# Places and nodes of edges compared by TensorE and ScalarE: a graph layer's gather loop on one core

## The chip, the cores and the metric

The kernel runs on one core of a Trainium2 chip. Its time is the device time of one execution in microseconds (us), as the median of several; before the change it is 2077.98 us over 9 runs (2075.69 to 2081.77). Profiles come from one execution each, by the hardware profiler. In them PE is TensorE's matmuls, PEld its weight loads, DVE is VectorE, ACT ScalarE, POOL GpSimd and SP SyncE, which here only issues DMAs.

## The reference

There are N = 12500 nodes with D = 128 features and M = 200000 edges, sorted by their destination `dst`; each has a source `src` and a weight. The reference, cut to what matters:

```
h = relu(layernorm(x))
Qv, Ku = h @ W_Q.T, h @ W_K.T
score = einsum('md,md->m', Qv[dst], Ku[src]) / sqrt(D) * exp(-edge_weight)
# of each dst keep the 16 edges with the highest scores; softmax over them -> alpha
agg = segment_sum(alpha * (h[src] @ W_msg.T), dst)
out = x + relu(h @ W_self.T + agg)
```

## The kernel before

The edges are cut into G = 112 groups of GC = 14 chunks with P = 128 edges each. A group's edges end at some 112 nodes in a row, so all its work is on one window of 128 nodes. A group also reads the first chunk of the next one, since a node's edges can reach into it: NJ = 15 chunks.

**Preparation** (lines 240 to 397). `src`, `dst` and the edge weights are loaded as rows (`src_r`, `dst_r`, `ew_r`: 121 rows of CPR = 13 chunks) and turned by TensorE into columns (`to_columns`, L256), one column to a chunk: `idx_all` (the source of each edge), `dec_all` (exp of minus the weight), `pos_all` (an edge's place within its node, from a scan, L366) and `dlw` (its node counted from the window's start, less an offset of 8 per chunk). The rows of x come in six parts on SP's queue (L274), are normed (`row_stats`, `normed`, `finish`) and stored as the table `h_tab` (L327). GpSimd gathers the rows of the sources by indirect DMAs, one for each chunk of 128 edges (`gather`, L168 to 174): of the first RAW = 4 groups from x itself (they are normed on the chip later, L491 to 495), then from `h_tab`. A group's rows lie in a tile `hs`, of which there are 7. Groups 0 to 6 are all issued here, with `idx_all` as the index.

**The loop** (L684 to 752) runs `i` from -3 to 117 and in each iteration calls stages for different groups, from `i + 3` (loads) to `i - 5` (output). The order of the calls is the order of the instructions on each engine; nothing reorders them. The stages that matter here:

- `load_dst` (SP): 1920 destinations of the group as int32, broadcast to all 128 partitions (`dstb`, 960 KB, two buffers).
- `far_of` and `to_edges` (ScalarE): `far = (dst - node)^2` for 128 nodes by 1920 edges, then `to_e = relu(1 - far)`, a matrix of ones and zeros in bf16 that brings nodes' values to edges by matmul.
- `places` (VectorE, L530 to 536): two comparisons on 128 edges by 15 chunks by 40. `ow` is one where an edge's node in its chunk's window of 40 nodes is `w` (L533), `po` where its place is `k` (L535).
- `q_to_edges` (TensorE, 45 matmuls in four parts), then `scores` (VectorE, one fused product with the gathered row for each chunk, L556), `scores_in_slots` (`sl = po * s`, L564), `slots_by_node` (TensorE, 15 matmuls with `ow`, L571) and `best` (VectorE, the 16 highest of 40 places for each node, L582 to 597).
- `kept_to_edges`, `on_edges`, `weights` (`alz = ow * kept`, L636), `sums` (TensorE, L646, into the PSUM bank `a`), `sums_turned`, `products`, `output` (L666), `store`.
- `let_go` (L464 to 473): for two chunks at a time VectorE copies their indices to a small tile `ix` and GpSimd issues their gathers. `more(k)` (L695) spreads a group's seven calls over an iteration, from group 7 on. The seventh group after has the same `hs` buffer, so the calls come after `sums` of the group that had it.

The call of the two stages that the change moves most, in the loop:

```
at(i, q_to_edges, 1)
at(i + 1, far_of)
at(i - 1, slots_by_node)
at(i + 1, places)
...
at(i - 3, sums, 0)
at(i - 2, kept_to_edges)
```

Of the kernel before, what the change touches and what calls it, by code (L numbers as in the profile page):

```python
# [20 lines left out]
P = 128  # L21
# [55 lines left out]
def gnn_layer(  # L77
# [38 lines left out]
    CPR = 13  # L116
# [4 lines left out]
    assert RR <= P and RR - RF <= 1  # L121
# [22 lines left out]
    nvec = const.tile([P, 1], F32, name="nvec")  # L144
    a_qk = const.tile([P, P], F32, name="a_qk")
    wselfT = const.tile([P, P], F32, name="wselfT")
    wmsgT = const.tile([P, P], F32, name="wmsgT")

    idx_all = const.tile([P, CW], I32, name="idx_all")
    dec_all = const.tile([P, CW], F32, name="dec_all")  # L150
    pos_all = const.tile([P, CW], F32, name="pos_all")
    dlw = const.tile([P, G, NJ], F32, name="dlw")

    nb = const.tile([P, G], F32, name="nb")
# [13 lines left out]
    def gather(g, j0, j1, index, table=h_tab):  # L168
        if j0 == 0:
            T[g]["hs"] = rows_pool.tile([P, GC, D], F32, name="hs", bufs=7)  # L170
        for j in range(j0, j1):
            nc.gpsimd.indirect_dma_start(  # L172
                out=T[g]["hs"][:, j, :], out_offset=None, in_=table[0:N, :],
                in_offset=bass.IndirectOffsetOnAxis(ap=index(j), axis=0))
# [4 lines left out]
    def load_dst(g):  # L179
        n = chunks[g] * P  # L180
        lo = g * EG
        T[g]["dstb"] = dstb = rows_pool.tile([P, NJ * P], I32, name="dstb", bufs=2)
        hi = min(lo + n, M)
        if hi < lo + n:
            nc.vector.memset(dstb[:, hi - lo:n], 1 << 21)
        nc.sync.dma_start(dstb[:, 0:hi - lo], dst[lo:hi].partition_broadcast(P))
# [47 lines left out]
    with tc.tile_pool(name="edges", bufs=1) as ep, ExitStack() as stage:  # L234
        prep = stage.enter_context(tc.tile_pool(name="prep", bufs=1))
        RL = HALO + RW

        src_r = ep.tile([RR, RL], I32, name="src_r")
        h0 = src_r.bitcast(F32)
        h1 = alz[0][0:RR, 0:RL]  # L240
        dst_all = alz[1][:, 0:CW]
        assert max(RL, CW) <= NJ * (WW + STEP)
        dst_r = ep.tile([RR, HALO + RW], I32, name="dst_r")
# [5 lines left out]

        def load_rows(t, a):  # L250
            if RF:
                nc.scalar.dma_start(t[0:RF, 0:RW], a[0:RF * RW].rearrange("(p c) -> p c", c=RW))
            if REM:
                nc.scalar.dma_start(t[RF:RF + 1, 0:REM], a[RF * RW:M].rearrange("(p c) -> p c", p=1))

        def to_columns(rows, lo, put):  # L256

            for j0 in range(0, CPR, 4):
# [5 lines left out]
                put(lambda t: t[:, 0:RR * CPR].rearrange("e (p j) -> e j p", j=CPR)[:, j0:j1, :],  # L264
# [3 lines left out]
        nc.vector.memset(src_r, 0)  # L268
        load_rows(src_r, src)
        xs, t = [], 0  # L270
        for i, n in enumerate(sizes):
# [4 lines left out]
            t += n  # L276
        make_identity(nc, ident)
        nc.gpsimd.iota(dst_r, pattern=[[1, RL]], base=1 << 21, channel_multiplier=0)
        nc.gpsimd.memset(dst_r[0:1, 0:HALO], -1)
        nc.gpsimd.iota(slots, pattern=[[1, KM]], base=0, channel_multiplier=0,  # L280
# [3 lines left out]
        nc.vector.memset(ew_r, 0.0)  # L284
# [8 lines left out]
        nc.vector.memset(pos_all[:, RR * CPR:CW], 0.0)  # L293
        nc.vector.memset(dec_all[:, RR * CPR:CW], 0.0)
        nc.vector.memset(dst_all[:, RR * CPR:CW], float(1 << 21))
        for j in range(NJ):
            nc.vector.memset(w0[:, j:j + 1], float(lead(j)))
        for k in range(2):
            nc.vector.memset(sl1[k][:, :, KM:], 1.0)
# [5 lines left out]
        to_columns(src_f, 0, lambda at, p: nc.vector.tensor_copy(at(idx_all), p))  # L305
# [3 lines left out]
        def finish(i):  # L309
            t0, n, xg = xs[i]  # L310
            normed(xg, n, *stat[i])
            if i == 1:
                for t, w in zip(ws, (w_q, w_k, w_self, w_msg)):
                    nc.scalar.dma_start(t, w)
                nc.scalar.dma_start(b_i[:, 1:G],
                                    bass.AP(dst.tensor, dst.offset + EG - 1, [[EG, 1], [EG, G - 1]]))

                nc.scalar.dma_start(dst_r[0:1, HALO:], dst[0:RW].rearrange("(p c) -> p c", p=1))
                if RF > 1:
                    nc.scalar.dma_start(dst_r[1:RF, :], bass.AP(dst.tensor, dst.offset + RW - HALO,  # L320
                                                                [[RW, RF - 1], [1, RL]]))
                if REM:
                    nc.scalar.dma_start(dst_r[RF:RF + 1, 0:HALO + REM],
                                        dst[RF * RW - HALO:M].rearrange("(p c) -> p c", p=1))
                load_rows(ew_r, ew)
            for a, b in cuts:
                nc.sync.dma_start(by_part(h_tab)[a:b, t0:t0 + n, :], xg[a:b])  # L327
            if i == 1:
                load_dst(0)
# [6 lines left out]
        for g in range(RAW, min(7, G)):  # L336
            gather_at_once(g, h_tab)
# [18 lines left out]
        nc.vector.tensor_copy(row_i[:, 1, G - TAIL:G], row[:, 3, 0:TAIL])  # L356
        pb = bank("s", 1)
# [5 lines left out]
        nc.vector.tensor_copy(dst_f, dst_r)  # L363
        nc.vector.memset(h0[:, 0:1], 0.0)
        nc.vector.tensor_tensor(h0[:, 1:RL], dst_f[:, 1:RL], dst_f[:, 0:RL - 1], op=OP.is_equal)
        nc.vector.tensor_tensor_scan(h1, h0, h0, 0.0, op0=OP.mult, op1=OP.add)  # L366
        bb = rows_pool.tile([P, 2, G], F32, name="bb")
        nc.vector.tensor_copy(bb, pb[:, 0:2 * G].rearrange("p (a g) -> p a g", a=2))
        nc.vector.tensor_scalar(nb, bb[:, 0, :], nvec, -1.0, op0=OP.add, op1=OP.mult)
        to_columns(dst_f, HALO, lambda at, p: nc.scalar.copy(at(dst_all), p))  # L370
        to_columns(h1, HALO, lambda at, p: nc.scalar.copy(at(pos_all), p))
# [6 lines left out]
        for k in range(2):  # L378
            nc.vector.memset(alz[k], 0.0)
# [550 lines left out]
```

## Time and profile before

| what | value |
|---|---|
| median of 9 runs | 2077.98 us |
| the profiled execution: its own time | 2084.66 us |
| the profiled execution: span from first to last instruction | 2082.8 us |
| mean granted clock of TensorE | 0.797 |
| busy: TensorE, VectorE, ScalarE, GpSimd | 1305.4, 1499.1, 659.4, 1545.3 us |
| bytes moved by DMA | 253 MB, 107 MB of them the broadcast of `dst` |
| one iteration of the loop | about 18 us |

A line of the page's groups, or of the trace's answers by line, has the source line, the engine, the operation, output <- inputs with shapes and a count; after the first bar the busy time in us and the mean of one in ns; after the second the idle time of that engine just before these instructions, and what ended most of it (`issue` is time in which the engine waited for nothing that the profile shows). A line of the timeline has the start in us from the span's start, the duration, the engine and the operation; in brackets the idle time before it. A line of the waits has the waiting engine and tile, what it waited for, the total in us, how many times, and the longest. "Granted clock" is the share of TensorE's full clock that it was given.

### The profile page before, as it was taken

How to read it: one execution, taken by the hardware profiler on the slowest of the kernel's cores; microseconds unless marked ns; L12 is line 12 of the kernel's file. 1: busy time of each engine (PE TensorE's matmuls, PEld its weight loads, DVE VectorE, ACT ScalarE, POOL GpSimd, SP SyncE). 2: the span in 40 equal slices, each digit the busy share in tenths (PEclk: the TensorE clock that was granted, in tenths of full speed). 3: DMA queues.
4: the chain of work that ended last, by engine and by line, in shares of the span. 5: the costliest groups of instructions: out<-in, count | busy, mean ns of one | idle time of the engine just before them, and what ended most of it. 6: DMA issues, size and time to landing. Idle time of an engine off the chain costs nothing. (4 is left out here: it accounts for less than half of the span.)

```text
span 2082.8 us, 43581 instructions
## 1 busy us (share of the span) xinstructions
PE 1305.4 (63%) x14574; PEld 1205.1 (58%) x14575; DVE 1499.1 (72%) x7420; ACT 659.4 (32%) x1306; POOL 1545.3 (74%) x1578
## 2 busy tenths in 40 slices
PE   0267776666666666666666666666666666666664
PEld 0156776555556666555565566665565655566664
DVE  5688887777767777777777667777777777777764
ACT  4772333222223323232233223232222232233220
POOL 3777777777777777777777777777777777777772
PEclk9878888777777787787787777778778777777778
DMA  8743444333334444433433334434443333433420
GB/s 189 242 136 118 151 129 133 121 114 110 117 117 121 120 121 122 121 120 114 118 113 118 118 120 121 121 120 121 121 118 114 116 117 119 119 120 121 120 67 23
DMA packets 117572, 253.17 MB, mean 122 GB/s; under 512 B 32798, under 2 KB 76065, under 8 KB 116576
## 3 DMA queue, kind: packets, MB, share of 16 engines
q1 hardware_dynamic: 66104, 144.92, 20.1%
q0 software_dynamic: 50144, 102.74, 19.6%
q10 hardware_dynamic: 1094, 2.69, 0.6%
q8 instruction: 115, 1.88, 0.4%
q14 instruction: 115, 0.94, 0.1%
HBM read 236.40 MB, written 14.40 MB: 120 GB/s over the span
## 5 line engine op out<-in xcount | busy, mean ns | idle before, releaser
L172 POOL DMA_INDIRECT hs<-h_tab,ix x1465 | 1430.3, 976 | 446.8 <-issue 319.6
L556 DVE SCALAR_TENSOR_TENSOR prod<-hs,dec_all,q 128x128 f32<-128x128 f32 x1674 | 511.4, 344 | 257.9 <-DMA hs<-h_tab,ix 251.6
L546 PE MATMUL q<-q,to_e 128*128 128x128 bf16 x5022 | 463.8, 254 | 23.6 <-DVE prod L556 22.7
L654 PE MATMUL s<-ident,agn 128*128 128x128 f32 x112 | 48.4, 432 | 627.7 <-DVE kept L635 627.2
L546 PEld LDWEIGHTS <-to_e 128*128 128x128 bf16 x5022 | 410.4, 116 | 45.0 <-issue 28.9
L646 PE MATMUL a<-hs,alz 128*128 128x128 f32 x3348 | 423.4, 280 | 1.3 <-DVE alz L636 1.3
L646 PEld LDWEIGHTS a<-hs,alz 128*128 128x128 f32 x3348 | 401.5, 196 | 1.9 <-DVE alz L636 1.9
L654 PEld LDWEIGHTS s<-ident,agn 128*128 128x128 f32 x112 | 19.9, 178 | 643.9 <-issue 642.1
L571 PE MATMUL e<-ow,sl 128*41 128x40 f32 x3348 | 249.4, 264 | 2.0 <-DVE sl L564 2.0
L571 PEld LDWEIGHTS e<-ow,sl 128*41 128x41 f32 x3348 | 234.0, 183 | 16.8 <-DVE sl L564 2.1
L522 ACT ACTIVATE far<-dstb,nb 128x1920 bf16<-128x1920 int32 x112 | 212.9, 1901 | 0.0
L527 ACT ACTIVATE to_e<-far 128x1920 bf16<-128x1920 bf16 x112 | 201.2, 1797 | 0.0
L658 ACT COPY aggT<-s 128x128 f32<-128x128 f32 x112 | 29.8, 266 | 504.1 <-PE s L654 504.1
L585 DVE TENSOR_SCALAR ell<-slots,e 128x40 f32<-128x40 f32 x112 | 29.3, 261 | 201.6 <-PE e L571 195.2
L602 ACT ACTIVATE e<-v,km 128x16 f32<-128x16 f32 x112 | 34.5, 308 | 352.0 <-DVE km L594 352.0
L556 DVE DVE_READ_ACCUMULATOR prod<-hs,dec_all,q 128x1 f32 x1674 | 138.1, 82 | 0.2
L472 DVE COPY ix<-idx_all 128x2 int32<-128x2 int32 (+1 forms) x733 | 127.9, 174 | 12.8 <-DMA hs<-h_tab,ix 6.7
L631 ACT ACTIVATE up<-up 128x15 f32<-128x15 f32 x112 | 24.0, 215 | 297.3 <-DVE up L623 297.3
L651 ACT ACTIVATE agn<-a,rden 128x128 f32<-128x128 f32 x112 | 41.2, 368 | 208.0 <-PE a L646 208.0
L172 POOL DMA_INDIRECT hs<-in_x_dram,idx_all x56 | 63.2, 1129 | 43.9 <-DVE idx_all L305 20.9
L564 DVE TENSOR_TENSOR sl<-po,s 128x600 f32<-128x600 f32 x112 | 87.5, 781 | 3.9
L636 DVE TENSOR_TENSOR alz<-ow,kept 128x600 f32<-128x600 f32 x112 | 87.5, 781 | 3.8
(166 smaller groups left out, 1621.6 us busy)
## 6 DMA issues: line engine op xcount, KB each, us to landing
dstb<-in_dst_dram SPq DMA_DIRECT2D x111, 960.0 KB
hs<-h_tab,ix POOLq DMA_INDIRECT x1465
h_r<-h_tab SPq DMA_DIRECT2D x112, 64.0 KB
x_t<-in_x_dram SPq DMA_DIRECT2D x108, 64.0 KB
out_dram<-o SPq DMA_DIRECT2D x108, 64.0 KB
xg<-in_x_dram SPq DMA_DIRECT2D x2, 1400.0 KB
h_tab<-xg SPq DMA_DIRECT2D x2, 1400.0 KB
xg<-in_x_dram SPq DMA_DIRECT2D x1, 1120.0 KB
```

Source lines behind the costliest of these rows:

```text
L172: nc.gpsimd.indirect_dma_start(out=T[g]["hs"][:, j, :], out_offset=None, in_=table[0:N, :], in_offset=bass.IndirectOffsetOnAxis(ap=index(j ...
L472: nc.vector.tensor_copy(ix[:, j0:j1], idx_all[:, GC * g + j0:GC * g + j1])
L522: nc.scalar.activation(T[g]["far"][:, 0:n], T[g]["dstb"][:, 0:n], AF.Square, bias=nb[:, g:g + 1])
L527: nc.scalar.activation(T[g]["to_e"][:, 0:n], T[g]["far"][:, 0:n], AF.Relu, bias=1.0, scale=-1.0)
L546: nc.tensor.matmul(pq[:, (j - j0) * P:(j - j0 + 1) * P], lhsT=T[g]["to_e"][:, j * P:(j + 1) * P], rhs=upper(T[g]["q"][:, k, :]), start=(k ...
L556: nc.vector.scalar_tensor_tensor(prod, rows_of(g, j), dec_all[:, c:c + 1], T[g]["pq", b][:, (j % 4) * P:(j % 4 + 1) * P], op0=OP.mult, op1 ...
L564: nc.vector.tensor_tensor(sl1[g % 2][:, 0:n, 0:KM], T[g]["po"][:, 0:n, :], bc(T[g]["s"][:, 0:n], KM), op=OP.mult)
L571: nc.tensor.matmul(et[0:KM + 1, STEP * j:STEP * j + WN], lhsT=sl1[g % 2][:, j, :], rhs=T[g]["ow"][:, j, :], start=False, stop=(j == n - 1))
L636: nc.vector.tensor_tensor(alz[g % 2].rearrange("e (j w) -> e j w", w=WW + STEP)[:, 0:n, 0:WN], T[g]["ow"][:, 0:n, :], bc(kept[:, 0:n], WN) ...
L646: nc.tensor.matmul(T[g]["pa"][:, 0:P], lhsT=alz[g % 2][:, WW * j + PRE:WW * j + PRE + P], rhs=rows_of(g, j), start=(j == 0), stop=(j == n ...
L651: nc.scalar.activation(T[g]["agn"], T[g]["pa"][:, 0:P], AF.Copy, scale=T[g]["rden"])
L654: nc.tensor.transpose(so[:, 2 * P:3 * P], T[g]["agn"], ident)
```

## The change

- `src`, `dst` and the weights are now rows of CPR = 14 chunks, so that row `g` is group `g`: 112 rows. They are loaded on SP's queue in parts with a multiple of 16 rows and a rest (`sixteens`), `src` first, ahead of x; weights of the layer, `dst` and edge weights behind x. Before, they were on ScalarE's queue.
- `rel` holds each row's destinations relative to the last one of the row before, in bf16, on the chip. The broadcast `load_dst` is gone: `far_of` spreads row `g` to 128 partitions by a matmul with a column of the identity (four parts of up to 512 edges), and ScalarE squares it from PSUM.
- `places` no longer runs on VectorE. For each group one matmul turns 32 columns of `pd` (places and nodes of its 15 chunks), a copy by ScalarE takes them to `pdT`, three matmuls with a constant matrix `minus_at` give "own value less slot" for 2 x 15 x 40 slots, ScalarE squares each part (`away`) and at the end takes `relu(1 - square)` for all 1200 in one instruction. All these matmuls write the one bank `a`, which `sums` uses too.
- `slots_by_node` is cut in three, between the parts of `far_of`; `kept_to_edges` moves ahead of `sums`.
- There are 8 `hs` buffers and `let_go` is moved ahead by an iteration; groups 4 to 7 are let go in pieces too, group 4 within the preparation.

The core of the diff:

```diff
-    CPR = 13
+    CPR = GC
...
-    pos_all = const.tile([P, CW], F32, name="pos_all")
-    dlw = const.tile([P, G, NJ], F32, name="dlw")
...
+    pd = const.tile([P, G, 2, 16], BF16, name="pd")
+    dlw = pd[:, :, 1, 0:NJ]
+    minus_at = const.tile([32, 2, NJ, KM], BF16, name="minus_at")
...
-            T[g]["hs"] = rows_pool.tile([P, GC, D], F32, name="hs", bufs=7)
+            T[g]["hs"] = rows_pool.tile([P, GC, D], F32, name="hs", bufs=8)
...
-    def load_dst(g):
...
+        def sixteens(a, b):
+
+            m = b - (b - a) % 16
+            return [(p, q) for p, q in ((a, m), (m, b)) if p < q]
+
         def load_rows(t, a):
-            if RF:
-                nc.scalar.dma_start(t[0:RF, 0:RW], a[0:RF * RW].rearrange("(p c) -> p c", c=RW))
+            for p0, p1 in sixteens(0, RF):
+                nc.sync.dma_start(t[p0:p1, 0:RW], a[p0 * RW:p1 * RW].rearrange("(p c) -> p c", c=RW))
...
+        nc.gpsimd.memset(alz[1], 0.0)
...
-        nc.vector.memset(pos_all[:, RR * CPR:CW], 0.0)
+        nc.vector.memset(pd, 1.0)
...
+        for w in range(2):
+            nc.vector.tensor_scalar(kk[:, 0:1], nvec[0:32, :], -16.0 * w, None, op0=OP.add)
+            nc.vector.tensor_scalar(kk[:, 1:2], kk[:, 0:1], 15.0, None, op0=OP.is_equal)
+            nc.vector.tensor_scalar(eq, jj, kk[:, 0:1], None, op0=OP.is_equal)
+            nc.vector.scalar_tensor_tensor(minus_at[:, w, :, :], bm(slots[0:32, :], NJ), kk[:, 1:2], eq,
+                                           op0=OP.mult, op1=OP.subtract)
+        nc.vector.memset(alz[0], 0.0)
...
+        let_go(RAW, 1)
+        nc.vector.tensor_scalar(rel, dst_f[:, HALO:], dst_f[:, HALO - 1:HALO], 1.0, op0=OP.subtract, op1=OP.subtract)
+        let_go(RAW, 2)
...
-        byg = dst_all.rearrange("e (g j) -> e g j", j=GC)
-        nc.vector.tensor_sub(dlw[:, :, 0:GC], byg[:, 0:G, :], bc(bb[:, 0, :], GC))
-        nc.vector.tensor_sub(dlw[:, :, GC], byg[:, 1:G + 1, 0], bb[:, 0, :])
-        nc.vector.tensor_tensor(dlw, dlw, bm(w0, G), op=OP.subtract)
-        for k in range(2):
-            nc.vector.memset(alz[k], 0.0)
...
-        def far_of(g):
-            n = chunks[g] * P
-            T[g]["far"] = win.tile([P, NJ * P], BF16, name="far", bufs=1)
-            nc.scalar.activation(T[g]["far"][:, 0:n], T[g]["dstb"][:, 0:n], AF.Square, bias=nb[:, g:g + 1])
+        def far_of(g, b):
+            n0, n1 = 4 * P * b, min(4 * P * (b + 1), chunks[g] * P)
...
+            pr = bank("a", 1)
+            nc.tensor.matmul(pr[:, 0:n1 - n0], lhsT=upper(ident[0:RR, g:g + 1]).to_broadcast([RR, P]),
+                             rhs=rel[:, n0:n1], start=True, stop=True)
+            nc.scalar.activation(T[g]["far"][:, n0:n1], pr[:, 0:n1 - n0], AF.Square, bias=minus)
...
+        def edges_turned(g):
+            pr = bank("a", 1)
+            nc.tensor.matmul(pr[0:32, 0:P], lhsT=pd[:, g, :, :].rearrange("e w j -> e (w j)"), rhs=upper(ident),
+                             start=True, stop=True)
+            T[g]["pdT"] = win.tile([32, P], BF16, name="pdT")
+            nc.scalar.copy(T[g]["pdT"], pr[0:32, 0:P])
+
+        def away(g, b):
+            if b == 0:
+                T[g]["aw"] = win.tile([P, 2 * NJ * KM], BF16, name="aw")
+            n0, n1 = 400 * b, 400 * b + 400
+            pr = bank("a", 1)
+            nc.tensor.matmul(pr[:, 0:400], lhsT=T[g]["pdT"],
+                             rhs=minus_at.rearrange("k w j s -> k (w j s)")[:, n0:n1], start=True, stop=True)
+            nc.scalar.activation(T[g]["aw"][:, n0:n1], pr[:, 0:400], AF.Square)
+
         def places(g):
-            n = chunks[g]
-            T[g]["ow"] = win.tile([P, NJ, WN], F32, name="ow", bufs=5)
-            nc.vector.tensor_tensor(T[g]["ow"][:, 0:n, :], bm(slots, n), bc(dlw[:, g, 0:n], WN), op=OP.is_equal)
-            T[g]["po"] = win.tile([P, NJ, KM], F32, name="po", bufs=4)
-            nc.vector.tensor_tensor(T[g]["po"][:, 0:n, :], bm(slots, n),
-                                    bc(pos_all[:, GC * g:GC * g + n], KM), op=OP.is_equal)
+            T[g]["opo"] = win.tile([P, 2, NJ, KM], F32, name="opo", bufs=4)
+            nc.scalar.activation(T[g]["opo"].rearrange("e w j s -> e (w j s)"), T[g]["aw"], AF.Relu, bias=1.0,
+                                 scale=-1.0)
+            T[g]["po"], T[g]["ow"] = T[g]["opo"][:, 0], T[g]["opo"][:, 1]
...
-            if i + 2 > 0:
-                at(i + 2, load_dst)
...
-                g, k = (i + 3, k + 2) if k < 5 else (i + 4, k - 5)
-                if 7 <= g < G:
+                if i in (-1, 0, 1):
+                    g = i + 6
+                else:
+                    g, k = (i + 4, k + 2) if k < 5 else (i + 5, k - 5)
+                    if g < 8:
+                        return
+                if i >= -1 and g < G:
                     let_go(g, k)
 
             at(i, q_to_edges, 0)
+            at(i + 1, edges_turned)
             at(i - 5, output)
             at(i - 5, store)
             at(i - 3, weights)
             more(0)
             at(i - 4, sums_turned)
+            at(i + 1, far_of, 0)
             at(i - 4, sums_turned_out)
             at(i + 1, q_out)
             at(i, q_to_edges, 1)
-            at(i + 1, far_of)
-            at(i - 1, slots_by_node)
-            at(i + 1, places)
+            at(i + 1, far_of, 1)
+            at(i - 1, slots_by_node, 0)
+            at(i + 1, far_of, 2)
+            at(i - 1, slots_by_node, 1)
+            at(i + 1, far_of, 3)
+            at(i - 1, slots_by_node, 2)
+            at(i + 1, away, 0)
...
             at(i, q_to_edges, 2)
+            at(i + 1, away, 1)
             at(i + 2, h_turned)
+            at(i + 1, away, 2)
...
+            at(i - 2, kept_to_edges)
             at(i - 3, sums, 0)
-            at(i - 2, kept_to_edges)
...
             more(5)
+            at(i + 1, places)
```

## The prediction

> **What bounds the kernel now.** I read the page's busy line first, then the costliest groups, then GpSimd's instructions in order of time, and beside them VectorE's.
>
> ```profile
> PE 1305.4 (63%) x14574; PEld 1205.1 (58%) x14575; DVE 1499.1 (72%) x7420; ACT 659.4 (32%) x1306; POOL 1545.3 (74%) x1578
> ...
> L172 POOL DMA_INDIRECT hs<-h_tab,ix x1465 | 1430.3, 976 | 446.8 <-issue 319.6
> L556 DVE SCALAR_TENSOR_TENSOR prod<-hs,dec_all,q 128x128 f32<-128x128 f32 x1674 | 511.4, 344 | 257.9 <-DMA hs<-h_tab,ix 251.6
> ```
>
> No engine looks full. But the second row's idle time is 446.8/1465 = 0.305 us before every gather, and it is the same 0.30 to 0.31 us whatever the releaser: it belongs to the instruction. Busy plus idle is 1.281 us a gather, 1877 us for 1465 of them. The third row says that VectorE, when it waits, waits for gathered rows. So GpSimd's stream of 1563 gathers is the bound. It runs without a gap from 53 us to 2044.8 us.
>
> ```profile
> 1911.72 0.95 POOL L172 DMA_INDIRECT hs<-h_tab,ix  x1 [0.30 <-issue]
> ...
> 1912.92 0.78 DVE L533 TENSOR_TENSOR ow<-slots,dlw 128x600 f32<-128x600 f32 x1
> 1912.97 1.54 POOL L172 DMA_INDIRECT hs<-h_tab,ix  x1 [0.30 <-DVE alz L636]
> ...
> 1913.62 0.78 DVE L535 TENSOR_TENSOR po<-slots,pos_all 128x600 f32<-128x600 f32 x1
> ...
> 1914.82 0.95 POOL L172 DMA_INDIRECT hs<-h_tab,ix  x1 [0.30 <-issue]
> ...
> 1925.70 0.77 DVE L625 TENSOR_TENSOR mine<-x,po 128x600 f32<-128x600 f32 x1
> ...
> 1926.08 0.95 POOL L172 DMA_INDIRECT hs<-h_tab,ix  x1 [0.31 <-issue]
> ```
>
> An undisturbed gather takes 0.946 us, 1.2505 us from start to start. One in each iteration takes more. The one at 1912.97 began while VectorE ran L533 and then L535 without a break, and ended 0.11 us after L535. This holds over the whole trace: a gather that starts while a VectorE operation with two SBUF inputs runs ends at least 0.82 us after that operation; it loses the operation's remainder less 0.13 us. L625, as long but with one input in PSUM, delays nothing. I put every slow gather after 168 us to the operation that ended 0.82 us before its end: L533 and L535 together carry 37 us, all others 5. From the group row, all of it is 1430.3 - 1465 x 0.946 = 44 us.
>
> **The two ends.**
>
> ```profile
> 20.16 1.03 DVE L303 CAST src_r<-src_r 121x1664 f32<-121x1664 int32 x1 [14.30 <-DMA src_r<-in_src_dram]
> ...
> 24.24 1.12 POOL L172 DMA_INDIRECT hs<-in_x_dram,idx_all  x1 [20.94 <-DVE idx_all L305]
> ...
> 46.55 0.95 POOL L172 DMA_INDIRECT hs<-in_x_dram,idx_all  x1 [3.67 <-DMA hs<-in_x_dram,idx_all]
> ...
> 110.73 1.29 POOL L172 DMA_INDIRECT hs<-h_tab,idx_all  x1 [0.30 <-issue]
> ...
> 2043.86 0.95 POOL L172 DMA_INDIRECT hs<-h_tab,ix  x1 [0.30 <-DVE km L594]
> ```
>
> The first gather waits for the sources, which land at 20.16 us beside the x loads. The 57th, first of group 4, starts at 110.73, the last at 2043.86, and 38.9 us of drain follow. So the span is 110.7 + 1506 x 1.2505 (1883.3) + 49.9 of delays + 38.9 = 2082.8 us. The profiled execution took 2084.66, 1.9 us over its span and 0.3% over the median 2077.98.
>
> **The change, part by part.**
>
> *Sources first, by sixteens.* The first 0.8 MB of SP's queue is now src, ahead of x. At the 217 GB/s of the first 20 us that is 3.7 us of transfer[...]. VectorE was free at 5.9. It loses two clears (1.50 and 1.45) and gains the fill of pd (3584 elements at L268's 0.87 ns, 3.1), the constant matrix (per half two small operations of 0.15, a comparison of some 0.4, a fused one of 0.78: 3.0 in all), and one alz clear (2.06): free at 11.2. So the cast starts near 11.4, and with the old 4.1 us from cast to gather the first one starts near 15.5: 8.7 earlier. The next 56 took 86.5 us: 70.0 of cadence, 6.2 of waits for landings (42.9 to 53 us), 10.2 of delays by VectorE. The delays by L375 and L377 (2.4) go, the scan's and L380's stay. The waits for landings could vanish or double, as more gathers now run beside the x loads; I keep 6. Gather 57: 15.5 + 70 + 6 + 7.5 = 99, against 110.7.
>
> *SP's order.* The h_tab stores now queue behind weights, dst and ew. The x loads held SP until 35.6; 1.9 MB more at 0.2 MB a us makes 45, and 6.4 MB of stores at the 337 GB/s of 60 to 80 us take 19: h_tab is done near 70, and gather 57 doesn't want it before 99. Cost nothing; without these 29 us of cover, the difference one for one. Group 4's copies (21 more of 0.17 us) sit among VectorE's preparation, which ended at 90 and should end near 70.
>
> *Places.* L533 and L535 (1.56 us an iteration, 173 in all) leave VectorE. Of the busy time nothing is gained, VectorE waits for rows anyway; of the port, 37 us. Here the Trainium skill speaks against me. "SBUF — State Buffer", the section on the shared port pair, says that tensor_tensor was seen not to stall GpSimd's DMA, as descriptor generation needs the write interface (inferred there); and also that an operation with two SBUF inputs contends with a GpSimd instruction that reads SBUF. By the first the change gains 0 here, by the second 37. An indirect gather reads its indices from SBUF, and the two rows above fit the second: I take 37.
>
> *What remains.* L564 (sl) and L636 (alz), 0.78 each, and L516 (0.6 for two) still hold the port. They now miss the gather starts narrowly: sl ends at +0.04 us from a start, alz at -0.04, since both follow the landing of the iteration's last row. That order stays. From below: 0 if the phases hold. From above: at random phase a 0.78 us window costs 0.24 and L516 0.14, so 0.62 an iteration, 70 us. I take 0.1 an iteration over 100 iterations, nearer the trace, and 8 for the first ten, which took 11: 18 us.
>
> *far_of, away, edges_turned.* Eight matmuls and eight ScalarE reads through one PSUM bank, so each waits for the one before. ScalarE rows give 0.31 + 0.83 ns per element with a bias operand (L522, both sizes) and 0.20 + 0.83 without (L527): four reads of 512 at 0.74, three of 400 at 0.54, opo 1.2, one of 0.25, less 1.91 for the old far: +4 us, ScalarE from 5.4 to 9.4 us of an iteration. TensorE has this gap:
>
> ```profile
> PE s L654 <- DVE kept L635: 627.2, 110, 6.8
> ```
>
> 5.7 us an iteration in which it waits for VectorE's output. The new matmuls take some 2 us of it. What counts is the chain that begins there, after `output`: sums_turned and the first 512 columns to 0.9 us, ScalarE to 1.6 and with its two old copies to 2.1, three more rounds of about 1.0, slots_by_node finished between them: best can start at 5.0 to 5.5, where it started at 4.1. From there to the next output VectorE was busy for 10.7 (14.0 less 3.3 of waits for rows). The sum is 16.0, and on TensorE: away and its reads to 9.5, sums, the q products and the rest 6.7 more: 16.2. The gathers need 17.5. So it fits, with 1.3 to spare.
>
> Rule and row again: "TensorE: Matmul & The Clock Gate", the part on psum-queue depth-cycling, says that short stalls on a PSUM queue can make the clock oscillate between full and half. The row: granted clock 0.797, halves after the 5.7 us gap. With the gap filled I expect 0.9 or more and 16.2; by the rule at half clock, TensorE's 13 us of work at full would grow, and the chain with it to about 18.2.
>
> *dst no longer broadcast.* 107 MB in 111 loads leave SP's queue. No gather waits for a landing after 53 us, so 0; it could shift landings, thus phases (above).
>
> *Eight buffers, earlier release.* GpSimd's gaps are 0.30 throughout, so no buffer is waited for: 0. Group 8's first gather is due near 169; its copy comes late in iteration 3. The first iterations grow to some 21 us (ScalarE's 5.5 of raw_normed now delays away), which puts it near 153: 16 us of cover.
>
> **Sum.** 99 + 1883.3 + 18 + 38.9 = 2039.2 of span, 43.6 less than before's; on the median 2034. The drain has no places or far in it and stays.
>
> **Rivals.** (A) As summed: 2010 (no waits or delays) to 2050; 58%. (B) The phases shift and sl, alz or q_parts meet gather starts: up to 70 us in place of 18, 2050 to 2085, middle 2065; the bare 0.08 us of margin speaks for it, the fixed order against; 16%. (C) The places aren't the cause, something at the iteration's start is (SP issues there too): 45 us of delays remain, only the start is gained, 2060; L625's row and the exact ends speak against; 10%. (D) The one-bank chain outgrows 17.5 us: iteration 3 would start near 145, and 109 iterations plus 26 of drain give 2155 span at 18.2, about 2150. It loses from 17.6 on. For it: single buffer, eight hand-overs that no row of before shows. Against: the sum; 16%.
>
> Numbers: under 2010 I leave 3%, over 2090 13%; range 2010 to 2090. About 0.2% is what a measurement can tell from no change: faster 80% (A, C and most of B), same 5%, slower 15%.
>
> **What would show it.** Gathers of 1.5 us gone, the group mean near 953 ns (0.1 us an iteration); first gather near 15.5, the 57th near 99; TensorE's wait before sums_turned near 1 us, clock over 0.9; VectorE still waiting for rows. Wrong if gaps over 0.31 appear on GpSimd after 60 us (D, or a late copy), or if slow gathers stay, now ending after L564, L636 or L516 (B) or after none (C).

## The result, and the profile after

The changed kernel takes 2058.2 us (median of 10 runs, 2057.6 to 2061.5) beside 2077.0 us for the kernel before (31 runs, 2071.1 to 2081.8): ratio 0.9911, interval 0.9901 to 0.9921. It is faster by 18.8 us, where 43.6 were forecast. The profiled execution took 2056.25 us with a span of 2054.5. In fifteen of the eighteen runs below TensorE, VectorE and ScalarE paused again and again with nothing to wait for, and the kernel before took 2690 to 2716 us beside them: of those only durations of single instructions and the order within the drain are read; their times are given but nothing is concluded from them.

The page of the changed kernel, its busy line and the rows that answer to those of before:

```profile
PE 1642.6 (80%) x15474; PEld 1294.0 (63%) x15475; DVE 1329.0 (65%) x7222; ACT 1041.0 (51%) x2198; POOL 1511.6 (74%) x1580
...
L176 POOL DMA_INDIRECT hs<-h_tab,ix x1507 | 1443.2, 958 | 472.3 <-issue 296.6
L591 DVE SCALAR_TENSOR_TENSOR prod<-hs,dec_all,q 128x128 f32<-128x128 f32 x1674 | 497.6, 344 | 147.5 <-DMA hs<-h_tab,ix 126.8
...
L690 PE MATMUL s<-ident,agn 128*128 128x128 f32 x112 | 39.3, 351 | 134.1 <-DVE o L702 130.4
```

The mean of the gathers falls from 976 to 958 ns. Their delays are 1443.2 - 1507 x 0.946 = 17.6 us, where they were 44. VectorE still waits for rows, 126.8 us. TensorE's wait for VectorE just before sums_turned (L690, L654 before) falls from 627 to 130 us, 1.2 an iteration.

GpSimd's instructions in order of time, the five that carry the sum (start, duration, idle before):

```profile
15.76 1.12 POOL L176 DMA_INDIRECT hs<-in_x_dram,idx_all  x1 [9.58 <-DVE idx_all L338]
...
94.99 0.94 POOL L176 DMA_INDIRECT hs<-h_tab,ix  x1 [0.30 <-issue]
...
165.08 2.31 POOL L176 DMA_INDIRECT hs<-h_tab,ix  x1 [0.30 <-issue]
180.32 2.50 POOL L176 DMA_INDIRECT hs<-h_tab,ix  x1 [12.93 <-ACT up L667]
...
2009.28 0.94 POOL L176 DMA_INDIRECT hs<-h_tab,ix  x1 [0.30 <-DVE km L631]
```

The fourth line is new. GpSimd stands still for 12.93 us, and the gather after it waits 0.26 us longer than usual. The one at 180.32 is the first of group 8. Its index copies (L191) come at 178.36 and 180.05 us. From the last line to the end of the span it is 2054.5 - 2009.3 = 45.2 us, where it was 38.9.

So the span is 95.0 + 1883.3 (1506 x 1.2505) + 17.6 of delays + 12.9 of stall + 45.2 = 2054.0, against 2054.5 measured. The forecast had 99 + 1883.3 + 18 + 0 + 38.9. Two of its terms hold within 0.5 us, the start is 4.0 better than forecast, and two fail, by 12.9 and 6.3.

### The profile page after: what moved, and what is told of

Same layout as the page of the kernel before. It is cut to its first block, busy times and chain, and to the rows that moved or that the text cites. A ratio compares the mean times of both kernels' runs of the same rounds, so it can differ in the third digit from the quotient of the medians.

```text
span 2054.5 us, 45456 instructions
## 1 busy us (share of the span) xinstructions
PE 1642.6 (80%) x15474; PEld 1294.0 (63%) x15475; DVE 1329.0 (65%) x7222; ACT 1041.0 (51%) x2198; POOL 1511.6 (74%) x1580
## 3 DMA queue, kind: packets, MB, share of 16 engines
q0 software_dynamic: 50144, 102.74, 19.8%
## 5 line engine op out<-in xcount | busy, mean ns | idle before, releaser
L176 POOL DMA_INDIRECT hs<-h_tab,ix x1507 | 1443.2, 958 | 472.3 <-issue 296.6
L591 DVE SCALAR_TENSOR_TENSOR prod<-hs,dec_all,q 128x128 f32<-128x128 f32 x1674 | 497.6, 344 | 147.5 <-DMA hs<-h_tab,ix 126.8
L682 PE MATMUL a<-hs,alz 128*128 128x128 f32 x3348 | 525.5, 321 | 10.3 <-ACT aw L565 0.4
L682 PEld LDWEIGHTS a<-hs,alz 128*128 128x128 f32 x3348 | 485.6, 230 | 21.1 <-ACT aw L565 17.6
L542 ACT ACTIVATE far<-a,minus 128x512 bf16<-128x512 f32 (+1 forms) x447 | 294.9, 660 | 335.7 <-PE a L540 325.4
L607 PEld LDWEIGHTS e<-opo,sl 128*41 128x41 f32 x3348 | 186.9, 139 | 100.7 <-issue 89.6
L540 PE MATMUL a<-rel,ident 112*128 112x512 bf16 (+1 forms) x447 | 193.1, 432 | 47.1 <-ACT far L542 24.5
L607 PE MATMUL e<-opo,sl 128*41 128x40 f32 x3348 | 228.3, 229 | 0.0
L565 ACT ACTIVATE aw<-a 128x400 bf16<-128x400 f32 x336 | 168.2, 501 | 104.0 <-PE a L563 103.2
L563 PE MATMUL a<-minus_at,pdT 32*128 32x400 bf16 x336 | 121.6, 362 | 122.7 <-ACT aw L565 108.2
L690 PE MATMUL s<-ident,agn 128*128 128x128 f32 x112 | 39.3, 351 | 134.1 <-DVE o L702 130.4
L569 ACT ACTIVATE opo<-aw 128x1200 f32<-128x1200 bf16 x112 | 136.1, 1215 | 0.0
L191 DVE COPY ix<-idx_all 128x2 int32<-128x2 int32 x754 | 125.7, 180 | 0.0
L690 PEld LDWEIGHTS s<-ident,agn 128*128 128x128 f32 x112 | 16.2, 145 | 147.6 <-DVE o L702 141.0
```

What stands on the lines that cost most here:

```text
L176: nc.gpsimd.indirect_dma_start(out=T[g]["hs"][:, j, :], out_offset=None, in_=table[0:N, :], in_offset=bass.IndirectOffsetOnAxis(ap=index(j ...
L191: nc.vector.tensor_copy(ix[:, j0:j1], idx_all[:, GC * g + j0:GC * g + j1])
L540: nc.tensor.matmul(pr[:, 0:n1 - n0], lhsT=upper(ident[0:RR, g:g + 1]).to_broadcast([RR, P]), rhs=rel[:, n0:n1], start=True, stop=True)
L542: nc.scalar.activation(T[g]["far"][:, n0:n1], pr[:, 0:n1 - n0], AF.Square, bias=minus)
L563: nc.tensor.matmul(pr[:, 0:400], lhsT=T[g]["pdT"], rhs=minus_at.rearrange("k w j s -> k (w j s)")[:, n0:n1], start=True, stop=True)
L565: nc.scalar.activation(T[g]["aw"][:, n0:n1], pr[:, 0:400], AF.Square)
```

## Experiments

**The start alone.** In the kernel before, only the sources go first in SP's queue:

```
-                nc.scalar.dma_start(t[0:RF, 0:RW], ...)
+                for p0, p1 in ((0, RF - RF % 16), (RF - RF % 16, RF)):
+                    eng.dma_start(t[p0:p1, 0:RW], ...)
...
-        load_rows(src_r, src)
+        load_rows(src_r, src, nc.sync)
```

> Edit: the kernel before, with the sources alone loaded first in SP's queue (its whole sixteens of rows, the rest of the rows, and the last part row), everything else as before. Theory (the first gather waits for the sources, which land late beside the x loads): the first gather starts at 15 to 17 us where it started at 24.24, the 57th 8 to 16 us earlier than 110.7, and as the gathers are the bound, the span is as much shorter: ratio to the kernel before 0.992 to 0.996. Rival (the start is hidden behind something later, the h_tab stores or VectorE's preparation): the 57th gather stays at 108 us or later, ratio 0.998 to 1.001. If TensorE holds the kernel back on this chip (the kernel before at 2690 us), the first gather shows the same and the time only part of it.

Measured: 2070.6 us (12 runs) beside 2077.3, ratio 0.9969, interval 0.9958 to 0.9980. GpSimd in that kernel, the first gather and the 57th:

```profile
13.54 1.12 POOL L172 DMA_INDIRECT hs<-in_x_dram,idx_all  x1 [10.25 <-DVE idx_all L306]
...
101.71 1.52 POOL L172 DMA_INDIRECT hs<-h_tab,idx_all  x1 [0.30 <-issue]
```

The first gather comes 10.7 us earlier, the 57th 9.0 earlier, and the time falls by 6.7 us. The profiled execution's drain is 40.9 us, 2.0 longer than that of before, with the order of the drain unchanged; 9.0 less 2.0 is 7.0. So the start gives nearly what the stream gains at the 57th gather, as it must where the stream is the bound. The ratio lies a little above what I expected: the drain moved by 2 us without an edit to it. The two profiled executions differ by more than the medians, 12.3 us of span: behind the 57th gather the stream of before's execution is 5.3 us longer (more on that in the section on the prediction).

**The port.** Three kernels. The first takes the places back to VectorE and leaves edges_turned, away and ScalarE's Relu out:

```
+            for w in (1, 0):
+                nc.vector.tensor_tensor(T[g]["opo"][:, w, 0:n, :], bm(slots, n), bc(pd[:, g, w, 0:n], KM),
+                                        op=OP.is_equal)
```

> Edit: the changed kernel with its places compared by VectorE again (two comparisons of 600 with two inputs in SBUF, where they stood before the change); edges_turned, away and ScalarE's Relu are left out. Theory (the port: a gather that starts during an operation with two SBUF inputs ends 0.82 us after it): one gather of each iteration takes about 1.5 us again, the group's mean is 970 to 978 ns where it is 958, 25 to 37 us of delays more; the first iterations are shorter without the away reads, so 5 to 13 us of the stall at 180 us go; net 2070 to 2085. Rival (the places weren't what delayed the gathers): mean 955 to 960 ns and 2045 to 2055. Rival (the new chain through one PSUM bank is what holds the changed kernel back): 2030 to 2045.

The second keeps the changed kernel whole and puts the same two comparisons, into a spare tile, where the old ones stood; the third puts two reductions there instead:

```
+                nc.vector.tensor_tensor(t[:, 0:n, :], bm(slots, n), bc(pd[:, g, w, 0:n], KM), op=OP.is_equal)
...
+                nc.vector.tensor_reduce(t, dec_all[:, 0:NJ * KM].rearrange("e (j k) -> e j k", k=KM),
+                                        axis=AX.X, op=OP.add)
```

> Edit: the changed kernel with the old places' two comparisons (600 elements, two inputs in SBUF, 0.78 us each) back on VectorE at their old place, their result unused; the places themselves still come from ScalarE. Theory (port): one gather of each iteration takes about 1.5 us again, the mean of the gathers rises from 958 to 978 to 990 ns, 30 to 50 us of delays more than without them. Rival (the place in the order or VectorE's load counts, not the inputs): the same delays show in the run with one-input operations of the same length. Rival (the gathers' delays had another cause): mean 950 to 960 ns.

> Edit: the changed kernel with two reductions of 600 elements with one input in SBUF (0.78 us each) at the same place, their result unused. Theory (port): no gather is delayed by them, mean 950 to 960 ns, the time within 5 us of the changed kernel's on the same chip. Rival (VectorE's load or its place counts): mean 978 ns or more, as with two inputs.

These three ran among the pauses: 2747.5 us beside 2712.9 for the first, and one execution each of the other two, 2741.8 and 2933.0 beside 2690.8. The groups with the two comparisons, which have two inputs in SBUF, under them the gathers, and one pair of both in order of time:

```profile
L578 DVE TENSOR_TENSOR spare<-slots,pd 128x600 f32<-128x600 f32 x222 | 173.1, 780 | 7.5 <-remote 2.6 <-PE q L272 1.0
...
L176 POOL DMA_INDIRECT hs<-h_tab,ix x1507 | 1483.0, 984 | 1059.4 <-DVE prod L597 418.0
...
1515.94 1.59 DVE L578 TENSOR_TENSOR spare<-slots,pd 128x600 f32<-128x600 f32 x2
1516.10 1.44 POOL L176 DMA_INDIRECT hs<-h_tab,ix  x1 [0.30 <-issue]
```

The same with the two reductions, which have one input:

```profile
L577 DVE TENSOR_REDUCE spare<-dec_all 128x15 f32<-128x600 f32 x224 | 173.5, 775 | 9.3 <-remote 3.3 <-ACT dec_all L402 2.2
...
L176 POOL DMA_INDIRECT hs<-h_tab,ix x1507 | 1430.1, 949 | 1302.8 <-DVE prod L597 668.9
...
1513.03 1.58 DVE L577 TENSOR_REDUCE spare<-dec_all 128x15 f32<-128x600 f32 x2
1513.19 0.94 POOL L176 DMA_INDIRECT hs<-h_tab,ix  x1 [0.30 <-issue]
```

Both add the same 173 us to VectorE at the same place. With two inputs the gathers' mean is 984 ns, with one 949: 1507 x 35 ns = 53 us of delays. In the lines above both gathers begin 0.16 us after the VectorE operation. Over the two traces, from the 57th gather on, 107 gathers begin while a comparison runs and take 1.43 us in the mean; 205 begin while a reduction runs and take 0.944, the longest 0.95. That the reductions write only 15 elements, and are another operation, is not what spares them: `mine` (L661) multiplies and writes 600 with one input in PSUM, and the 89 gathers that begin beside it in the changed kernel take 0.944 us too. The kernel with the places taken back has 987 ns, raw_late and kept_back, which have neither, 948 and 950. Undisturbed, the kernels with the places on VectorE have 971 to 976 (before, start_only, kept_first), those without 951 and 958. So the second input in SBUF is the cause of these delays, and rival (C) falls. As in the prediction, the row and the Trainium skill's page "SBUF — State Buffer" ("Who interferes with whom") differ in part: the page saw tensor_tensor not stall GpSimd's DMA, and here it delays the gathers; that two inputs in SBUF contend with GpSimd's reads, and that tensor_reduce doesn't, is what 984 and 949 ns show.

**The drain.** One line of the change, alone in the kernel before:

```
-            at(i - 3, sums, 0)
             at(i - 2, kept_to_edges)
+            at(i - 3, sums, 0)
```

> Edit: the kernel before with this one line of the change alone, kept_to_edges ahead of the first half of the sums in TensorE's order. Theory (in the drain all 30 sums then wait for best): the two intervals between the third and the fifth last but one output, 6.8 and 6.0 us before, become 10.0 and 7.5, the drain 38.9 becomes 43 to 45 us, nothing else moves; where the kernel before takes 2077 us, 2081 to 2083, ratio 1.002 to 1.003. Rival (the longer drain comes from the one-bank chain, which this kernel hasn't): intervals and time as before, ratio 0.999 to 1.001. On a chip where the kernel before takes some 2700 us, the intervals show the same, since TensorE has little to do in the drain.

Measured: 2084.8 us (8 runs) beside 2078.4, ratio 1.0037, interval 1.0024 to 1.0050. So this line costs 6.4 us by the medians, 7.7 (5.0 to 10.4) by the ratio; 4 to 6 were expected. TensorE in the drain of that kernel:

```profile
2045.33 0.55 PE L614 MATMUL x<-km,to_e 128*128 128x43 bf16 x15 [2.14 <-DVE km L597]
2045.72 5.22 PE L646 MATMUL a<-hs,alz 128*128 128x128 f32 x30
...
2054.63 0.52 PE L614 MATMUL x<-km,to_e 128*128 128x43 bf16 x9 [2.47 <-DVE km L597]
2054.97 6.18 PE L646 MATMUL a<-hs,alz 128*128 128x128 f32 x30
```

And in the drain of start_only, which has the order of before:

```profile
2045.57 1.83 PE L647 MATMUL a<-hs,alz 128*128 128x128 f32 x14 [0.51 <-DVE alz L637]
2047.53 0.40 PE L615 MATMUL x<-km,to_e 128*128 128x43 bf16 x9
2047.77 2.03 PE L647 MATMUL a<-hs,alz 128*128 128x128 f32 x16
```

The changed kernel's drain has the pattern of kept_first:

```profile
2019.56 0.55 PE L650 MATMUL x<-km,to_e 128*128 128x43 bf16 x15 [2.14 <-DVE km L633]
2019.95 5.22 PE L682 MATMUL a<-hs,alz 128*128 128x128 f32 x30
```

With the changed order TensorE stands idle for 1.9 to 2.5 us until VectorE's best has made km, and then all 30 matmuls of the sums follow. With the old one, 14 of them run while VectorE works, and kept_to_edges waits for 0.4 us at most. The two intervals between the starts of the fifth last, the fourth last and the third last `output` are 6.8 and 6.0 us in before, 9.0 and 6.0 in start_only, 10.0 and 7.5 in the changed kernel, 10.0 and 10.2 in kept_first. The drain of kept_first is 48.2 us, more than the 43 to 45 expected; its stream is not longer (1925.4 us from the 57th to the last gather, 1927.9 in start_only), so the line costs nothing ahead of the drain.

The line was also put back in the changed kernel, alone and with the next experiment's edit:

> Edit: kept_to_edges back behind the first half of the sums in TensorE's order, as before the change. Theory (the drain grew from 38.9 to 45.2 us because all 30 sums of the last groups now wait for best, where 14 of them used to run beside it): the drain is 39 to 40 us, the time 5 to 6 us less, 2052 to 2053, and the cadence of the gathers from 700 us on stays 1.251 us. Rival (the drain grew by the one-bank chain itself): drain 44 to 46 us and 2058. Rival (the sums then wait for the last away read in the shared bank, and the iteration outgrows 17.5 us): cadence over 1.26 us, time 2065 or more.

> Edit: both edits, raw_normed behind the third away read and kept_to_edges behind the first half of the sums. Theory: the two are independent, one at the start and one at the end, and their gains add: 9 to 13 and 5 to 6, time 2039 to 2044, GpSimd without a gap over 4 us after 100 us and a drain of 39 to 40 us. Rival (the stream of gathers isn't the bound any more, some other chain takes over): less than 10 us in all.

They took 2991 and 2991 us, with the kernel before at 2713. In the drain TensorE has little to do, and there the two intervals are 6.8 and 6.0 us in both runs of kept_back and in three of six of both (7.8, 7.8 and 9.0 beside 6.0 in the others). The sum of the two intervals is 12.7 to 15.0 us in all ten profiles with the old order and 17.1 to 20.3 in all ten with the changed one. So the line is the cause of most of the 6.3 us in the changed kernel too: 17.5 against 12.7 makes 4.8 of them. That putting it back would give 5 to 6 us of time there is worked out, not measured.

**The stall at 180 us.** raw_normed goes from between the first and second away read to behind the third:

```
             at(i + 1, away, 0)
-            if i + 1 < RAW:
-                at(i + 1, raw_normed)
...
             at(i + 1, away, 2)
+            if i + 1 < RAW:
+                at(i + 1, raw_normed)
```

> Edit: in the four first iterations the normalisation of the raw rows stands after the third away read in ScalarE's order, not between the first and the second. Theory (the first iterations are too long because 5.5 us of raw_normed sit inside the one-bank chain, so group 8's index copies come at 178 us where 167 are due): the copies come at 163 to 168 us, the 12.9 us stall of GpSimd at 180 shrinks to 0 to 4 us, everything after it starts that much earlier; time 2058 less 9 to 13, so 2045 to 2049. Rival (the first iterations are long because of VectorE's preparation, row statistics and checks, and the bank chain is only beside it): the copies stay within 3 us of 178, time 2055 to 2059. Rival (GpSimd's stream is no longer the bound): the stall goes and the time stays.

It took 2957 us beside 2713, and the pauses hide the stall. The same kernel again:

> The same kernel as raw_late, because the runs beside which it stood, the kernel before's among them, took 2713 us on that chip where they took 2077 before. If the kernel before takes 2072 to 2082 us here, the theories are those of raw_late: raw_normed off the one-bank chain gives 2045 to 2049 us and no stall of GpSimd over 4 us at 180 us, or 2055 to 2059 if VectorE's work sets the first iterations. If the kernel before takes some 2710 us again, TensorE is the bound there, and this one takes 2950 to 2960.

2918 us beside 2690, with pauses too. Four kernels once more:

> The kernel of raw_late where the kernel before takes 2077 us. Theory (raw_normed inside the one-bank chain makes the first iterations long): group 8's index copies come at 163 to 168 us, not 178; the 12.9 us stall of GpSimd at 180 shrinks to 0 to 4; 2045 to 2049 us, ratio to the kernel before 0.984 to 0.987. Rival (VectorE's statistics, checks and comparisons make them long): copies within 3 us of 178, 2055 to 2059 us, ratio 0.990 to 0.992.

> The kernel of kept_back where the kernel before takes 2077 us. Theory (all 30 sums of the last groups wait for best, where half of them ran beside it): the drain is 39 to 40 us, not 45.2; cadence 1.251 us; 2052 to 2053 us, ratio 0.988 to 0.989. Rival (the one-bank chain itself lengthens the drain): 44 to 46 us, 2058. Rival (the sums wait for the last away read in the shared bank and the iteration outgrows 17.5 us): cadence over 1.26 us, 2065 or more.

> The kernel of both where the kernel before takes 2077 us. Theory: the gains add, 9 to 13 and 5 to 6: 2039 to 2044 us, ratio 0.982 to 0.984. Rival: the sums now lengthen the first iterations as much as raw_normed's move shortens them, 2050 or more.

> The kernel of undo_places where the kernel before takes 2077 us. Theory (port): the gathers' mean rises from 958 to 978 to 990 ns, 30 to 48 us of delays; the first iterations are shorter without the away reads, 5 to 13 us of the stall go; 2075 to 2098 us. Rival (the places didn't delay the gathers): mean 955 to 960 ns, 2045 to 2055 us. Rival (the away chain holds the changed kernel back): 2030 to 2045 us.

2956, 2995, 2990 and 2750 us beside 2715, with pauses. The gathers' mean with the places taken back is 985 ns here, and kept_back's intervals are 6.8 and 6.0 us as before. Four more runs of both:

> The kernel of both, once more, for a chip on which the kernel before takes 2077 us. Theory (raw_normed in the one-bank chain makes the first iterations long, kept_to_edges ahead of the sums lengthens the drain): group 8's index copies come at 163 to 168 us, GpSimd stalls 0 to 4 us there instead of 12.9; the drain is 39 to 41 us instead of 45.2, with 12.7 us instead of 17.5 between the third and the fifth last but one output; 2039 to 2044 us, ratio to the kernel before 0.982 to 0.984. Rival (VectorE's work makes the first iterations long): a stall of 10 us or more stays and 2050 to 2053 us, ratio 0.987 to 0.989. Where the kernel before takes some 2700 us: 2985 to 2995, as in the two runs before.

> The kernel of both a fourth time, as for both_3: where the kernel before takes 2077 us, a stall of 0 to 4 us at 180 us, a drain of 39 to 41 us and 2039 to 2044 us (theory), or a stall of 10 us or more and 2050 to 2053 us (rival: VectorE's work makes the first iterations long); where the kernel before takes some 2700 us, 2980 to 2995.

> The kernel of both a fifth time, as for both_3: where the kernel before takes 2077 us, a stall of 0 to 4 us at 180 us, a drain of 39 to 41 us and 2039 to 2044 us (theory), or a stall of 10 us or more and 2050 to 2053 us (rival: VectorE's work makes the first iterations long); where the kernel before takes some 2700 us, 2960 to 2995.

> The kernel of both a sixth time, as for both_3: where the kernel before takes 2077 us, a stall of 0 to 4 us at 180 us, a drain of 39 to 41 us and 2039 to 2044 us (theory), or a stall of 10 us or more and 2050 to 2053 us (rival: VectorE's work makes the first iterations long); where the kernel before takes some 2700 us, 2960 to 2995.

2985 us beside 2713, 2965 beside 2691, 2993 beside 2716, 2964 beside 2692. Of the theories only the drain's intervals can be read; the second of these times lies under the 2980 to 2995 foreseen. The two runs that had shown no pauses, start_only and kept_first, had a kernel with fewer instructions, so the move was made in a shorter one. It leaves out the last six of each group's fifteen blocks of the sums, so it does not compute the layer:

```
             half = n // 2
+            n = min(n, 9)
             for j in range(half) if part == 0 else range(half, n):
```

> Edit: raw_normed behind the third away read, as in raw_late, and the sums over only the first nine of each group's fifteen blocks of edges: the last six blocks' share of the sums is left out, 12 of TensorE's matmuls an iteration, so that the kernel has fewer instructions than the kernel before (all seven kernels with more than that met an engine stall in every iteration, the two of the kernel before's length did not). Theory (raw_normed in the one-bank chain makes the first iterations long): group 8's index copies come at 160 to 168 us, not 178; GpSimd stalls 0 to 4 us there, not 12.9; the last gather starts at 1994 to 2002 us, not 2009; with a drain of 40 to 43 us, as its sums are shorter, 2036 to 2045 us. Rival (VectorE's statistics, checks and comparisons make them long): copies within 3 us of 178, last gather at 2006 or later, 2050 to 2056 us. If the number of instructions is not what stalls the engines, the kernel before takes some 2700 us here again.

(The kernels with pauses were six in fifteen runs, not seven.) Measured: 2041.4 us (5 runs) beside 2076.5, ratio 0.9830, interval 0.9816 to 0.9844. GpSimd around 170 us:

```profile
165.28 0.94 POOL L176 DMA_INDIRECT hs<-h_tab,ix  x1 [0.30 <-issue]
173.41 0.94 POOL L176 DMA_INDIRECT hs<-h_tab,ix  x1 [7.18 <-DVE prod L591]
176.47 1.44 POOL L176 DMA_INDIRECT hs<-h_tab,ix  x1 [2.12 <-issue]
```

The copies come at 172.39, 6.0 us earlier than in the changed kernel but not at 160 to 168; 1.0 of the 6.0 is the loop's earlier beginning (first pdT at 84.49, not 85.46). The stall is 6.9 + 1.8 = 8.7 us, where it was 12.9. The shorter sums have no part in this: the first of them that is cut short begins at 171.81, on TensorE, and nothing ahead of the copies waits for it. So the normalisation in the chain makes some of the stall, but not most of it as the theory had it, and the rival, that the copies stay within 3 us of 178, fails as well. The reason shows in one of the changed kernel's first iterations, ScalarE's instructions:

```profile
122.98 0.24 ACT L556 CAST pdT<-a 32x128 bf16<-32x128 f32 x1
...
129.80 0.50 ACT L565 ACTIVATE aw<-a 128x400 bf16<-128x400 f32 x1 [0.71 <-PE a L563]
130.20 5.48 ACT L220 ACTIVATE hs<-hs,smr,rsr 128x128 f32<-128x128 f32 x14
135.59 0.24 ACT L612 COPY eT<-e 41x128 f32<-41x128 f32 x1
135.73 0.49 ACT L565 ACTIVATE aw<-a 128x400 bf16<-128x400 f32 x1
...
137.20 1.79 ACT L547 ACTIVATE to_e<-far 128x1920 bf16<-128x1920 bf16 x1
...
145.28 0.24 ACT L556 CAST pdT<-a 32x128 bf16<-32x128 f32 x1
```

and the same stretch of raw_late_light, ScalarE and TensorE:

```profile
129.57 0.50 ACT L565 ACTIVATE aw<-a 128x400 bf16<-128x400 f32 x1 [0.41 <-PE a L563]
129.97 5.48 ACT L220 ACTIVATE hs<-hs,smr,rsr 128x128 f32<-128x128 f32 x14
...
135.35 1.79 ACT L547 ACTIVATE to_e<-far 128x1920 bf16<-128x1920 bf16 x1
137.04 0.25 ACT L517 COPY hT<-s 128x128 f32<-128x128 f32 x1
...
137.34 0.80 PE L520 MATMUL s<-a_qk,hT 128*128 128x128 f32 x2 [7.00 <-ACT hT L517]
...
139.68 0.25 ACT L556 CAST pdT<-a 32x128 bf16<-32x128 f32 x1 [1.18 <-PE a L553]
```

After the move the away reads no longer wait for the 5.48 us of raw_normed (L220), but to_edges and hT do, TensorE waits 7.00 us for hT, and the next edges_turned stands behind that product. Read from these lines, it is a loop through ScalarE's own order, and the normalisation is in it wherever it stands ahead of hT. The first four iterations take 17.6, 19.9, 22.3 and 19.8 us in the changed kernel, and 18.3, 19.4, 17.5 and 19.6 after the move. To put it behind hT was not tried, so that this explains the rest of the stall is not shown.

The last gather starts 14.9 us earlier than in the changed kernel, at 1994.4. Of that, 4.2 are the shorter stall, 1.0 an earlier 57th gather (94.0), and 1433.6 against 1443.2 us of gathers makes 9.6 of fewer delays. Most of the delays stand where the loop catches up with rows that are there already: in both kernels its iterations then take 15.4 us (mostly 14.8 to 16.1, until about 620 us), so VectorE's sl and alz drift through the starts of the gathers, which are 17.5 us apart by the group. This is not the stall's doing: before and start_only have no stall and catch up too, until about 320 us. In the changed kernel the gathers that end 0.82 us after sl carry 10.1 us of delays and those after alz 5.8, all but 3.2 of them before 700 us; in raw_late_light 3.9 and 2.1. Why it loses less at the same pace was not tested, so the 9.6 us can't be put down to the move.

## Why the prediction was right in sign and wrong in size

The measured 2058.2 us lie above (A)'s 2010 to 2050, and in (B)'s 2050 to 2085 and near (C)'s 2060 by chance only: neither mechanism came.

*What bounds the kernel*: right. From 700 to 1900 us a gather starts every 1.2503 to 1.2519 us, and VectorE waits for rows.

*Sources first*: right. First gather 15.76 (15.5 forecast), 57th 94.99 (99): waits among the 56 gathers make 3.5 us instead of 6, and VectorE's delays 5.6 instead of 7.5. The cast starts at 11.71 (11.4 forecast).

*Places*: right in cause, as two_in and one_in show. *What remains*: 17.6 us where 18 stood, in part by luck. An undisturbed gather takes 0.944 us in this execution, not 0.946, and by that the delays are 21 us, while the cadence is 1.2485 us and makes 3 us less. And they come in another way than thought: not 0.1 an iteration throughout, but mostly in the catching up, with 3 us in twelve gathers after 700 us. The 70 us set as the upper bound, which rival (B) took over, is too high by the prediction's own rule: a loss of the remainder less 0.13 us makes 0.17 for each of sl and alz and 0.09 for L516 at random phase, 0.43 an iteration, 48 us in all. In the steady part sl mostly ends too soon after a gather's start to cost much, VectorE and GpSimd of the changed kernel:

```profile
1511.34 0.79 DVE L599 TENSOR_TENSOR sl<-opo,s 128x600 f32<-128x600 f32 x1
1511.95 0.99 POOL L176 DMA_INDIRECT hs<-h_tab,ix  x1 [0.30 <-issue]
...
1512.51 0.78 DVE L672 TENSOR_TENSOR alz<-opo,kept 128x600 f32<-128x600 f32 x1
...
1513.24 0.95 POOL L176 DMA_INDIRECT hs<-h_tab,ix  x1 [0.30 <-issue]
```

The gather at 1511.95 begins 0.18 us before sl ends and loses 0.04, as the rule of 0.82 us from the end has it.

*far_of, away, edges_turned*: right. Where the gathers don't hold it back, before 620 us, an iteration takes 15.4 us; 16.0 to 16.2 were forecast. The clock is 0.868, under the 0.9 I expected but up from 0.797 (0.92 and 0.91 in the stretches from 200 to 400 and from 400 to 700 us, 0.83 to 0.85 from 700 to 1900), so the 18.2 us that I had worked out at half clock from "TensorE: Matmul & The Clock Gate" (psum-queue depth-cycling) didn't come, and neither did rival (D).

*Eight buffers, earlier release*: this step failed. It said "its copy comes late in iteration 3 ... near 153: 16 us of cover". It comes at 178.4. The length of the first iterations was right, 79.6 us for four where 84 were reckoned. Wrong was where they begin, 85.5 us (the first pdT) and not near 70: VectorE's preparation ends at 78.0, and ScalarE still copies pd and dec_all from 72.2 to 83.9, for which the prediction had no term. And the copies stand another 13.3 us into iteration 3: by the prediction's own figures, 70 and four of 21, iteration 3 begins at 154, so a copy late in it can't come at 153. 85.5 + 79.6 + 13.3 = 178.4. So 16 us of cover were a stall of 12.9.

*The drain "stays"*: this step failed. I had looked for places and far in it and not at the one line of the change that swaps kept_to_edges and the sums. In the steady part it costs nothing (the streams of kept_first and start_only are alike); in the drain nothing else is left to fill TensorE's wait. The drain is 6.3 us longer here, most of it by this line, which costs 6.4 to 7.7 us of time alone in the kernel before.

*The sum set against the median*: the third miss, 9 us. The forecast took the 43.6 us from the median. But the profiled execution of before was 6.7 us above the median that I used, and after the change the profiled execution is 2.0 us below its median. Some 3.8 us of the 6.7 are undisturbed gathers that took longer: 1.2510 us from start to start in before's execution, 1.2485 in those of the changed kernel, start_only and kept_first (1506 x 0.0025). The delays beyond that hardly differ between the executions with the places on VectorE: 49 us from the 57th gather on in before, 48 in start_only, 45 in kept_first. Why undisturbed gathers differ between executions stays open. In all: 15.3 of span (stall, drain and start), 6.7 and 2.0 make 24.0 of the 24.2 us between 2034 and 2058.2.

## What to carry to other kernels

Where a stream bounds a kernel, follow the change to the stream's two ends: check when its first refill is issued, by adding up the first iterations from their true start, and what each changed line does once nothing fills the waits any more. A reordering that is free in the steady state can be paid in the drain. Before a difference worked out in one profiled execution is taken from a median, see how far that execution lies from the median, and where.

## What the hardware showed that I had not expected

A gather is delayed where the VectorE operation beside it has two inputs in SBUF, not by the operation's length alone: gathers' mean 984 ns against 949, for operations of 780 and 775 ns.

The pauses of fifteen runs: for example VectorE in the second run of raw_late, independent instructions of 0.29 us that begin 1.4 us apart with nothing waited for, at a granted clock of 1.00:

```profile
100.90 0.29 DVE L200 BATCH_NORM_STATS2 str<-hs 128x6 f32<-128x128 f32 x1 [1.10 <-issue]
102.30 0.29 DVE L200 BATCH_NORM_STATS2 str<-hs 128x6 f32<-128x128 f32 x1 [1.11 <-issue]
103.69 0.30 DVE L200 BATCH_NORM_STATS2 str<-hs 128x6 f32<-128x128 f32 x1 [1.09 <-issue]
```

They came with every experiment of 44,335 instructions or more and with none of 43,585 or fewer, on the same chip too, and slowed the kernel before, with its 43,581, beside them by 30%. The changed kernel itself, with 45,456, was recorded without them. They cost the kernels unlike amounts: two_in took 2741.8 us and one_in, with two instructions fewer, 2933.0. What brings them on stays open.
